# Mamba scan units of one channel chunk by four states, the last image's B products by TensorE and GpSimd, and three quarters of the corner weighting on ScalarE, in a two-layer vision kernel

## The chip, the core and the metric

The kernel runs on one core of a Trainium2 chip. The metric is device time in microseconds of one execution. Engine names as the profile has them: PE is TensorE, PEld its weight loads, DVE is VectorE, ACT is ScalarE, POOL is GpSimd, SP is SyncE (which only issues DMAs here). All arithmetic is float32.

## The reference, cut to what matters

The input is four images of 128 x 128 pixels with 128 channels.

Layer 0, on the group-normalised image: for each of two channel groups, a 3 x 3 convolution gives an offset for each of nine taps; the image is sampled at the nine moved places with bilinear weights (four corners); the 9 x 64 samples go through a depthwise 3 x 3 convolution and a pointwise one to 64 channels. The result is added to the image.

Layer 1, on the group-normalised result: every image row is a sequence of 128 steps for two Mamba layers in a row. One layer, for a sequence, with 256 inner channels d and 16 states n:

```
xz = h @ in_w ; u, res = split(xz)
u = silu(causal_conv4(u) + cb)
dt, B, C = split(u @ xw)
delta = softplus(dt @ dtw + dtb)
h[d,n](t) = exp(delta[d](t) * A[d,n]) * h[d,n](t-1) + delta[d](t) * u[d](t) * B[n](t)
y[d](t) = sum over n of h[d,n](t) * C[n](t) + u[d](t) * D[d]
out = (y * silu(res)) @ ow
```

That result is added too.

## The kernel before, in words

**Order of the work.** `layer0(0)` convolves image 0 alone, and beside it makes the statistics and sampling tables of images 1 to 3 (`todo`). Then the main loop steps two generators: `layer1()`, the Mamba work on image b, and `layer0(b + 1)`, the convolution of the next image. A step of layer 1 is one *unit*; one image has 32 blocks of four rows x 2 layers x 8 units = 512 units. The 288 steps of a layer 0 (32 strips of four rows x nine slot pairs) are spread over all but the last 24 units. Image 3 has Mamba work with no convolution beside it. The program order of this loop goes to a scheduler, which orders each engine's instructions within what the tiles' dependences allow; every engine then works through its own list in order.

**Layer 0, one step** (`gather` and `sample`, lines 347 to 402). Eight indirect DMAs, issued by POOL, fetch for two halves h of two rows each the four corners of 128 pixels for two taps (`gt`, four buffers, two per step). `sample` multiplies each corner by its weight into `gw`: half h = 0 by one DVE tensor_tensor of 128 x 1024 (L387), half h = 1 by 16 ACT activations of 128 x 64 (L382). PE turns and sums the corners into PSUM (`add_transposed`, L128), ACT copies them to one of four `s` buffers (L401), and `add_up` multiplies by the weights on PE (L420). `prep` computes offsets and weights of eight rows (48 times beside layer 1); `table_part` scales the image into the table that is gathered from (`xt`, `xg`; L215, L220).

**Layer 1, the part ahead of a block** (`pre`): projections on PE, `silu` and `softplus` on ACT. At its end four DVE operations of 128 x 1024 (L588 to L591) make delta and du = delta * u. B and C are written to DRAM (`bcd`) so that they can be loaded again, broadcast to all partitions, in `main`.

**Layer 1, one unit, images 0 to 2** (`main`, the `else` branch). A unit is two states (NQ) of both channel chunks (NC), 2,048 elements a partition. SP loads B and C of two states, 128 x 1024 each (`bc`, two buffers each). ACT makes exp(delta * A) with four activations of 128 x 508 (L627) into one of three `da` buffers. DVE makes hs = du * B in two operations of 128 x 1024 (L661), runs the recurrence as one tensor_tensor_scan of 128 x 2048 (L667), and multiplies by C (L670). PE adds the 16 turned pieces into y (L128).

**Layer 1, one unit, image 3** (`in_last`). du is turned by PE (`turn_du`), multiplied by B as a per-partition scalar into `xs`, half by POOL (L646) and half by ACT (L644), turned back by PE into PSUM (`px`, L651), and DVE runs four scans of 128 x 512 that read PSUM (L653) and one multiplication by C (L656).

**End of a block**: DVE multiplies y by silu(res) (L677), PE turns it and projects it, ACT copies.

Of the kernel before, what the change touches and what calls it, by code (L numbers as in the profile page):

```python
# [31 lines left out]
XP = DTR + 1 + 2 * NS  # L32

# [30 lines left out]
def block_kernel(ctx: ExitStack, tc: tile.TileContext, a: dict, out: bass.AP):  # L64
# [26 lines left out]
    pb = ctx.enter_context(tc.tile_pool(name="l0b", bufs=1))  # L91
    ps = ctx.enter_context(tc.tile_pool(name="l0ps", bufs=2, space=PSUM))
    psa = ctx.enter_context(tc.tile_pool(name="l0psa", bufs=2, space=PSUM))
# [3 lines left out]
    psy = ctx.enter_context(tc.tile_pool(name="l1psy", bufs=1, space=PSUM))  # L97

# [6 lines left out]
    offw = loadw("offw", [P, NT, 64])  # L105
# [10 lines left out]
    ones = cw.tile([P, P], F32, name="ones")  # L116
    nc.vector.memset(ones, 1.0)

    wc = cw.tile([P, NT, NT, CG], F32, name="wc")
# [43 lines left out]
    cvw = loadw("cvw", [P, NL, DCONV, NC * P], pool=p2, tag="hs")  # L163
# [7 lines left out]
    xn = cw.tile([P, RB + 2, WP], F32, name="xn")  # L171
    nc.vector.memset(xn, 0.0)

    NSB = 4
    sbuf_s = [cw.tile([P, 4, WP], F32, name=f"s{i}") for i in range(NSB)]
# [5 lines left out]
    def stats_part(b, j):  # L181
        if j == 0:
            stats[b] = small.tile([P, NJ, 6], F32, tag="stats", name=f"stats_{b}")
        xr = pb.tile([P, 4, P], F32, tag="xr", name=f"xr_{b}_{j}", bufs=2)
        nc.sync.dma_start(xr, x[b, 4 * j : 4 * j + 4].rearrange("r w c -> w r c"))
        pt4 = ps.tile([P, 4, P], F32, tag="t", name=f"pt4_{b}_{j}")
        for i in range(4):
            nc.tensor.transpose(pt4[:, i, :], xr[:, i, :], ident)
        nc.vector.bn_stats(stats[b][:, j, :], pt4.rearrange("p r w -> p (r w)"))

    def norm_part(b):
# [3 lines left out]
        for nm, v in (("s", scale), ("b", bias)):  # L195
# [4 lines left out]
            row = small.tile([P, P], F32, tag=f"row_{nm}", name=f"row_{nm}_{b}")  # L200
# [6 lines left out]
    def table_part(b, j):  # L207
# [4 lines left out]
        xt = pb.tile([P, 5, P], F32, tag="xt", name=f"xt_{b}_{j}", bufs=2)  # L212
# [4 lines left out]
        xg = pb.tile([P, G, 5, CG], F32, tag="xg", name=f"xg_{b}_{j}", bufs=1)  # L217
# [150 lines left out]
    def sample(b, j, u, gts):  # L368
# [3 lines left out]
        for h in range(2):  # L372
# [4 lines left out]
            if h:  # L377

                for r in range(2):
                    for s in range(4):  # L380
                        for v in range(2):
                            nc.scalar.activation(  # L382
                                gw[:, r, s, v], gts[h][:, v, r, s * CG : (s + 1) * CG], AF.Copy,
                                scale=wt[:, u, r0 + r, s, v : v + 1],
                            )
            else:
                nc.vector.tensor_tensor(  # L387
                    gw.rearrange("p r s v c -> p (r s) v c"),
                    gts[h].rearrange("p v r (s c) -> p (r s) v c", c=CG),
                    wv.unsqueeze(3).to_broadcast([P, 8, 2, CG]),  # L390
# [75 lines left out]

    NDA = 3
    das = [cw.tile([P, NC, NQ, SR, P], F32, name=f"da{i}") for i in range(NDA)]
    zero = cw.tile([P, NC * NQ * SR], F32, name="zero")
    nc.vector.memset(zero, 0.0)  # L470
    n_da = [0]

# [20 lines left out]
    duts = []  # L493
    n_dut = [0]

    def turn_du(st, nm):

        if not duts:
            duts.append(p2.tile([P, 2, SR, NC * P], F32, tag="hs", name="duts"))
        n_dut[0] += 1  # L500
        dut = duts[0][:, n_dut[0] % 2]
        for k in range(SR // 2):
            pt = ps1.tile([P, 2, NC, P], F32, tag="t", name=f"pdu_{nm}_{k}")
            for i in range(2):
                for c in range(NC):
                    o = (2 * k + i) * P
                    nc.tensor.transpose(pt[:, i, c, :], st["du"][:, c, o : o + P], ident)
            nc.scalar.copy(dut[:, 2 * k : 2 * k + 2], pt.rearrange("p s c d -> p s (c d)"))  # L508
        st["dut"] = dut

    def pre(st, l):

        blk = st["blk"]
        nm = f"{blk}_{l}"
# [45 lines left out]
        if in_last(blk):  # L560

            pbt = ps1.tile([P, SR, XP], F32, tag="t", name=f"pbt_{nm}")
            for i in range(SR):
                nc.tensor.transpose(pbt[:, i, :], dbl[:, i * P : (i + 1) * P], ident[0:XP, 0:XP])
            st["bt"] = p2.tile([P, SR, NS], F32, tag="bt", name=f"bt_{nm}", bufs=2)
            nc.scalar.copy(st["bt"], pbt[:, :, DTR + 1 : DTR + 1 + NS])
# [4 lines left out]
        du = p2.tile([P, NC, TB], F32, tag="du", name=f"du_{nm}", bufs=2)  # L571
# [11 lines left out]
        nc.scalar.activation(du, w1, AF.Ln)  # L583
        nc.scalar.activation(w1, w1, AF.Identity, bias=-1.0)
# [3 lines left out]
        nc.vector.tensor_tensor(e, w1, e, ALU.subtract)  # L588
        nc.vector.tensor_tensor(de, de, e, ALU.subtract)
        nc.vector.tensor_tensor(de, de, du, ALU.add)  # L590
        nc.vector.tensor_tensor(du, de, u, ALU.mult)  # L591
        st.update(u=u, g=g, delta=de, du=du, bcd=bcd)
        st.pop("dut", None)
        if in_last(blk) and duts:
            yield
            turn_du(st, nm)

    def main(st, l):

        blk = st["blk"]  # L600
        nm = f"{blk}_{l}"

        y = psy.tile([P, SR, NC, P], F32, tag="y", name=f"y_{nm}")
# [6 lines left out]
        if in_last(blk) and "dut" not in st:  # L610
            turn_du(st, nm)
        for q in range(NS // NQ):
            bc = []
            for w in range(in_last(blk), 2):
# [208 lines left out]
```

## Time and profile before

| what | us |
|---|---|
| timed runs, median of 3 | 25,891.06 (25,885.81 to 25,894.32) |
| profiled execution, first to last instruction (span) | 24,903.2 |
| difference of the two | 987.9 |
| setup, statistics and table of image 0 | 0 to 273 |
| convolution of image 0 alone | 273 to 3,311 |
| Mamba of images 0 to 2 with convolution of images 1 to 3 | 3,311 to 20,573 |
| Mamba of image 3 | 20,573 to 24,903 |
| busy over the span: PE / DVE / ACT / POOL | 80% / 84% / 65% / 72% |

The timed runs count from start to end of the execution, the span from the first to the last instruction that the profiler recorded; the profiled execution has no timed figure of its own. In the profile a group is all instructions of one line, engine, operation and tiles; it has their number, the busy time, the mean duration in ns, and the time for which the engine stood idle ahead of them, with what ended that idle time. A wait is put down to what came last. POOL's indirect DMAs are counted as busy from issue until their descriptors are out; the data land later.

### The profile page before, as it was taken

How to read it: one execution, taken by the hardware profiler on the slowest of the kernel's cores; microseconds unless marked ns; L12 is line 12 of the kernel's file. 1: busy time of each engine (PE TensorE's matmuls, PEld its weight loads, DVE VectorE, ACT ScalarE, POOL GpSimd, SP SyncE). 2: the span in 40 equal slices, each digit the busy share in tenths (PEclk: the TensorE clock that was granted, in tenths of full speed). 3: DMA queues.
4: the chain of work that ended last, by engine and by line, in shares of the span. 5: the costliest groups of instructions: out<-in, count | busy, mean ns of one | idle time of the engine just before them, and what ended most of it. 6: DMA issues, size and time to landing. Idle time of an engine off the chain costs nothing. (4 is left out here: it accounts for less than half of the span.)

```text
span 24903.2 us, 331178 instructions
## 1 busy us (share of the span) xinstructions
PE 19986.7 (80%) x121156; PEld 13946.7 (56%) x121156; DVE 20935.3 (84%) x13018; ACT 16107.7 (65%) x38037; POOL 17956.4 (72%) x11270
## 2 busy tenths in 40 slices
PE   5788788888888878888888878888888877878877
PEld 3555455555555555555555555555555556666666
DVE  2221269999999999999999999999999998888888
ACT  2444466666666666666666666666666667888887
POOL 4777777887887857788887866787887845555555
PEclk8999989999999888999999888999999889999999
DMA  4554544454444444454544444454454442222221
GB/s 136 157 159 130 151 142 157 156 161 158 158 159 156 158 145 153 157 162 157 159 161 155 159 150 151 153 163 158 159 160 157 157 138 67 69 69 71 70 69 68
DMA packets 1530815, 3471.82 MB, mean 139 GB/s; under 512 B 243283, under 2 KB 717651, under 8 KB 1529052
## 3 DMA queue, kind: packets, MB, share of 16 engines
q1 hardware_dynamic: 1086812, 2242.08, 28.0%
q0 software_dynamic: 442368, 1208.55, 15.4%
q8 instruction: 951, 15.58, 0.3%
q14 instruction: 684, 5.60, 0.1%
HBM read 3299.19 MB, written 150.47 MB: 139 GB/s over the span
## 5 line engine op out<-in xcount | busy, mean ns | idle before, releaser
L359 POOL DMA_INDIRECT gt<-table,idx x9216 | 15606.0, 1693 | 4665.8 <-issue 2582.2
L627 ACT ACTIVATE da<-de,aneg 128x508 f32<-128x508 f32 x8192 | 5455.4, 711 | 2609.2 <-PE y L128 2357.7
L667 DVE TENSOR_TENSOR_SCAN da<-da,hs 128x2048 f32<-128x2048 f32 x1536 | 6792.2, 4422 | 120.2 <-ACT da L627 23.8
L128 PE MATMUL y<-ident,da 128*128 128x128 f32 x32768 | 4753.9, 306 | 2176.1 <-DVE da L670 1901.2
L420 PE MATMUL acc<-s,wc 128*64 128x256 f32 (+3 forms) x38400 | 6060.3, 439 | 276.7 <-ACT s L401 269.1
L128 PEld LDWEIGHTS y<-ident,da 128*128 128x128 f32 x32768 | 4247.0, 159 | 2997.4 <-DVE da L670 2050.8
L382 ACT ACTIVATE gw<-gt,wt 128x64 f32<-128x64 f32 x18432 | 4613.2, 337 | 1024.2 <-DMA gt<-table,idx 592.1
L420 PEld LDWEIGHTS acc<-s,wc 128*64 128x64 f32 x38400 | 3200.8, 140 | 2440.1 <-issue 1287.5
L128 PE MATMUL p<-ident,gw 128*128 128x128 f32 x18432 | 2896.6, 305 | 1471.5 <-DVE gw L387 1215.5
L646 POOL TENSOR_SCALAR xs<-duts,bt 128x256 f32<-128x256 f32 x2048 | 2349.7, 1164 | 2249.2 <-ACT duts L508 1185.7
L661 DVE SCALAR_TENSOR_TENSOR hs<-du,ones,bc 128x1024 f32<-128x1024 f32 x3072 | 3828.0, 1281 | 0.0
L670 DVE SCALAR_TENSOR_TENSOR da<-da,ones,bc 128x2048 f32<-128x2048 f32 x1536 | 3609.6, 2350 | 31.8
L128 PEld LDWEIGHTS p<-ident,gw 128*128 128x128 f32 x18432 | 2363.9, 157 | 2272.0 <-DVE gw L387 1150.1
L387 DVE TENSOR_TENSOR gw<-gt,wt 128x1024 f32<-128x1024 f32 x1152 | 1403.7, 1219 | 2357.9 <-DMA gt<-table,idx 1883.7
L653 DVE TENSOR_TENSOR_SCAN da<-da,px 128x512 f32<-128x512 f32 x2048 | 2350.6, 1202 | 509.2 <-PE px L651 509.2
L401 ACT COPY s<-p 128x512 f32<-128x512 f32 x1152 | 669.7, 581 | 2102.5 <-PE p L128 2100.1
L530 PE MATMUL pu<-hp,inc 128*128 128x512 f32 x4096 | 1830.4, 594 | 1.1 <-ACT ot L700 0.8
L651 PE MATMUL px<-ident,xs 128*128 128x128 f32 x8192 | 1213.5, 287 | 537.8 <-DVE da L653 322.1
L651 PEld LDWEIGHTS px<-ident,xs 128*128 128x128 f32 x8192 | 972.2, 147 | 818.0 <-POOL xs L646 329.3
L530 PEld LDWEIGHTS pu<-hp,inc 128*128 128x128 f32 x4096 | 747.8, 190 | 813.1 <-issue 809.3
L656 DVE TENSOR_TENSOR da<-da,bc 128x2048 f32<-128x2048 f32 x512 | 1172.0, 2289 | 6.6
L644 ACT ACTIVATE xs<-duts,bt 128x256 f32<-128x256 f32 x2048 | 894.3, 499 | 19.3 <-PE px L651 18.8
(133 smaller groups left out, 14768.7 us busy)
## 6 DMA issues: line engine op xcount, KB each, us to landing
bc<-bcd SPq DMA_DIRECT2D x3584, 512.0 KB
gt<-table,idx POOLq DMA_INDIRECT x9216
table<-xg SPq DMA_DIRECT2D x1016, 64.0 KB
xt<-in_x SPq DMA_DIRECT2D x124, 320.0 KB
xr<-in_x SPq DMA_DIRECT2D x128, 256.0 KB
x<-xo SPq DMA_DIRECT2D x128, 256.0 KB
x1t<-x SPq DMA_DIRECT2D x128, 256.0 KB
x1t_o<-x SPq DMA_DIRECT2D x128, 256.0 KB
```

The lines of the kernel that those rows point to most:

```text
L128: nc.tensor.matmul(o, v, ident, is_transpose=True, start=start, stop=stop, skip_group_check=True)
L359: nc.gpsimd.indirect_dma_start(out=gt[:, v, r], out_offset=None, in_=flat, in_offset=bass.IndirectOffsetOnAxis(ap=idx[:, ri, o : o + 1], a ...
L382: nc.scalar.activation(gw[:, r, s, v], gts[h][:, v, r, s * CG : (s + 1) * CG], AF.Copy, scale=wt[:, u, r0 + r, s, v : v + 1],)
L420: nc.tensor.matmul(accs[b, j + i0][CG * g : CG * g + CG, q : q + rb - ra, :], wc[sl, v, e, :], st[p + 4 * g if p < 4 else 8][sl, ra:rb, kx ...
L530: nc.tensor.matmul(px.rearrange("p (s t) -> p s t", s=SR), inc[:, l, j, c * P : (c + 1) * P], h[:, :, j : j + P], start=(j == 0), stop=(j ...
L627: nc.scalar.activation(da[:, c, n, :, 1:], dv[:, :, 1:], AF.Exp, scale=aneg[:, l, c, s : s + 1])
L646: nc.gpsimd.tensor_scalar(xs[:, i], st["dut"][:, i], bv, None, ALU.mult)
L651: nc.tensor.transpose(px[:, i, :], xs[:, i, c * P : (c + 1) * P], ident)
L653: nc.vector.tensor_tensor_scan(dn, dn, px.rearrange("p s t -> p (s t)"), 0.0, ALU.mult, ALU.add)
L661: nc.vector.scalar_tensor_tensor(hs[:, :, n, :], st["du"], ones[:, 0:1], bc[0][:, n].unsqueeze(1).to_broadcast([P, NC, TB]), op0=ALU.mult, ...
L667: nc.vector.tensor_tensor_scan(df, df, hs.rearrange("p c n t -> p (c n t)"), 0.0, ALU.mult, ALU.add)
L670: nc.vector.scalar_tensor_tensor(dc, dc, ones[:, 0:1], cv, op0=ALU.mult, op1=ALU.mult)
```

## The change

**Units of layer 1** are now one chunk by four states (NU) instead of both chunks by two states; there are still eight to a block and layer. hs is one operation of 128 x 2048. B and C are loaded every second unit, 128 x 2048 each, two buffers each. ACT's subtraction of 1 (L584) is folded into the first DVE operation of the preamble, and the product du is made in `make_du`, ahead of the last scan of the block before.

**Corner weighting.** For images 1 to 3 DVE keeps one of the four rows of a step (128 x 512) and ACT takes three (24 activations instead of 16). For image 0 DVE takes all four rows (two operations of 128 x 1024) and ACT none.

**Last image.** du of chunk 0 is reordered into four groups of 32 steps, turned by PE, and 16 matmuls of 32 rows per four states multiply it by a masked B (`make_d` on POOL, `fill` on PE), straight into PSUM; du of chunk 1 is multiplied by the broadcast B on POOL (`times_b`, 128 x 2048). DVE then runs one scan of 128 x 2048 per unit, from PSUM for chunk 0 and from SBUF for chunk 1, and one multiplication by C. The exponentials are made two units ahead in four buffers. B is loaded for this image as well.

**Memory.** The pools of layer 0 lie on the right side and are released ahead of the last image; a pool `first` holds the tables' tiles (`xt` four buffers instead of two, `xg` two instead of one) and is released when layer 1 begins. `s` has three buffers instead of four.

The diff, cut:

```diff
-    NSB = 4
-    sbuf_s = [cw.tile([P, 4, WP], F32, name=f"s{i}") for i in range(NSB)]
+    NSB = 3
+    sbuf_s = [l0w.tile([P, 4, WP], F32, name=f"s{i}") for i in range(NSB)]
...
-        xt = pb.tile([P, 5, P], F32, tag="xt", name=f"xt_{b}_{j}", bufs=2)
+        xt = pp.tile([P, 5, P], F32, tag="xt", name=f"xt_{b}_{j}", bufs=4)
...
-        xg = pb.tile([P, G, 5, CG], F32, tag="xg", name=f"xg_{b}_{j}", bufs=1)
+        xg = pp.tile([P, G, 5, CG], F32, tag="xg", name=f"xg_{b}_{j}", bufs=2)
...
-            if h:
-
-                for r in range(2):
-                    for s in range(4):
-                        for v in range(2):
-                            nc.scalar.activation(
-                                gw[:, r, s, v], gts[h][:, v, r, s * CG : (s + 1) * CG], AF.Copy,
-                                scale=wt[:, u, r0 + r, s, v : v + 1],
-                            )
-            else:
+            alone = 2 if b == 0 else 0 if h else 1
+            for r in range(alone, 2):
+                for s in range(4):
+                    for v in range(2):
+                        nc.scalar.activation(
+                            gw[:, r, s, v], gts[h][:, v, r, s * CG : (s + 1) * CG], AF.Copy,
+                            scale=wt[:, u, r0 + r, s, v : v + 1],
+                        )
+            if alone:
                 nc.vector.tensor_tensor(
...
+                    gw[:, 0:alone].rearrange("p r s v c -> p (r s) v c"),
+                    gts[h][:, :, 0:alone].rearrange("p v r (s c) -> p (r s) v c", c=CG),
+                    wv[:, 0 : 4 * alone].unsqueeze(3).to_broadcast([P, 4 * alone, 2, CG]),
                     ALU.mult,
                 )
...
+    def load_bc(st, u):
+
+        bc = []
+        for w in range(2):
+            t = lm["pool"].tile([P, NU, TB], F32, tag=f"bc{w}", name=f"bc{w}_{st['nm']}_{u}", bufs=2)
+            n0 = w * NS + u * NU
+            nc.sync.dma_start(t, st["bcd"][n0 : n0 + NU, :].partition_broadcast(P))
+            bc.append(t)
+        st["bc", u] = bc
...
-        nc.scalar.activation(du, w1, AF.Ln)
-        nc.scalar.activation(w1, w1, AF.Identity, bias=-1.0)
+        ln = p2.tile([P, NC, TB], F32, tag="yg", name=f"ln_{nm}")
+        nc.scalar.activation(ln, w1, AF.Ln)
...
-        nc.vector.tensor_tensor(e, w1, e, ALU.subtract)
+        nc.vector.scalar_tensor_tensor(e, w1, -1.0, e, op0=ALU.add, op1=ALU.subtract)
         nc.vector.tensor_tensor(de, de, e, ALU.subtract)
-        nc.vector.tensor_tensor(de, de, du, ALU.add)
-        nc.vector.tensor_tensor(du, de, u, ALU.mult)
+        nc.vector.tensor_tensor(de, de, ln, ALU.add)
...
+    def main(st, l, nst, nl):
...
+        for k in range(NC * NS // NU):
+            u, c = divmod(k, NC)
+            if c == 0:
+                load_bc(st, u)
...
+            nc.scalar.copy(da.rearrange("p n s t -> p (n s) t")[:, :, 0], zero)
+            dv = st["delta"][:, c].rearrange("p (s t) -> p s t", s=SR)
+            for i in range(NU):
+                n = u * NU + i
+                nc.scalar.activation(da[:, i, :, 1:], dv[:, :, 1:], AF.Exp, scale=aneg[:, l, c, n : n + 1])
+            hs = lm["pool"].tile([P, NU, TB], F32, tag="hs", name=f"hs_{nm}_{k}")
+            nc.vector.scalar_tensor_tensor(
+                hs, st["du"][:, c].unsqueeze(1).to_broadcast([P, NU, TB]), one, st["bc", u][0],
+                op0=ALU.mult, op1=ALU.mult,
+            )
+            if k == NC * NS // NU - 1 and nst and not in_last(nst["blk"]):
+                make_du(nst)
+            df = da.rearrange("p n s t -> p (n s t)")
+            nc.vector.tensor_tensor_scan(df, df, hs.rearrange("p n t -> p (n t)"), 0.0, ALU.mult, ALU.add)
+            nc.vector.scalar_tensor_tensor(df, df, one, ct, op0=ALU.mult, op1=ALU.mult)
...
+    def make_d(st, u):
+
+        d = le["r"].tile([P, SR, NU, QW], F32, tag="D", name=f"D_{st['nm']}_{u}", bufs=3)
+        nc.gpsimd.tensor_tensor(
+            d, st["bt"][:, :, NU * u : NU * u + NU].unsqueeze(3).to_broadcast([P, SR, NU, QW]),
+            le["mask"].unsqueeze(1).unsqueeze(1).to_broadcast([P, SR, NU, QW]), ALU.mult,
+        )
...
+    def fill(st, u):
+
+        px = le["ps"].tile([P, SR, NU, P], F32, tag="dbu", name=f"px_{st['nm']}_{u}")
+        for q in range(SR):
+            for g in range(SR):
+                o = slice(g * QW, (g + 1) * QW)
+                nc.tensor.matmul(
+                    px[:, g, :, q * QW : (q + 1) * QW],
+                    st["dut"][o, q], st["D", u][o, q],
+                    start=True, stop=True, skip_group_check=True,
+                )
...
+    def times_b(st, u):
+
+        t = le["r"].tile([P, SR, NU, P], F32, tag="dbu", name=f"dbu_{st['nm']}_{u}", bufs=2)
+        nc.gpsimd.tensor_tensor(
+            t, st["du1"].rearrange("p (s t) -> p s t", s=SR).unsqueeze(2).to_broadcast([P, SR, NU, P]),
+            st["bc", u][0].rearrange("p n (s t) -> p s n t", s=SR), ALU.mult,
+        )
...
+    def main_last(st, l, nst, nl):
...
+            hs = le["r"].tile([P, SR, NU, P], F32, tag="he", name=f"he_{nm}_{k}", bufs=3)
+            src = st.pop(("dbu", u)) if c else st["px"]
+            nc.vector.tensor_tensor_scan(
+                hs.rearrange("p s n t -> p (s n t)"),
+                st.pop(("da", k)).rearrange("p s n t -> p (s n t)"),
+                src.rearrange("p s n t -> p (s n t)"), 0.0, ALU.mult, ALU.add,
+            )
+            if c == 0 and nxt[0]:
+                fill(*nxt)
+            nc.vector.tensor_tensor(
+                hs, hs, st["bc", u][1].rearrange("p n (s t) -> p s n t", s=SR), ALU.mult
+            )
...
```

## The prediction

> **What bounds the kernel now.** I read the stages first, then the groups of one stage, then its instructions in order of time. The table by stage (columns: us, then busy time and count of PE, PEld, DVE, ACT, POOL, then clock, DMA share, GB/s) has convolution alone, convolution of images 1 to 3 beside Mamba blocks, and Mamba of the last image:
>
> ```profile
> 273.00:3300.00 3027.00, 2455.94 (x15578) 1546.96 (x15580) 673.52 (x1020) 1345.87 (x5035) 2315.12 (x2314) 0.90 0.50 144
> 3311.00:20573.00 17262.00, 13999.52 (x83687) 9655.16 (x83686) 16357.04 (x8941) 11283.44 (x26768) 13282.61 (x6894) 0.90 0.48 156
> 20573.00:24903.00 4330.00, 3466.47 (x21606) 2703.64 (x21604) 3804.24 (x2876) 3467.19 (x6206) 2349.73 (x2048) 0.93 0.21 69
> ```
>
> The middle stage is 69% of the span and DVE is busy 95% of it. That alone says "shorten DVE". But look at POOL, which issues the gathers. The groups of 500 to 3,100 us, then of 3,800 to 8,600 us (count | busy us, mean ns | idle before):
>
> ```profile
> L359 POOL DMA_INDIRECT gt<-table,idx x1987 | 1990.5, 1002 | 610.9 <-issue 567.6 <-DMA gt<-table,idx 16.5 <-ACT gw L382 14.9
> ...
> L359 POOL DMA_INDIRECT gt<-table,idx x2012 | 3878.8, 1928 | 922.3 <-issue 560.4 <-DVE gw L387 234.2 <-ACT gw L382 82.2
> L667 DVE TENSOR_TENSOR_SCAN da<-da,hs 128x2048 f32<-128x2048 f32 x424 | 1874.9, 4422 | 34.0 <-ACT da L627 7.9 <-DVE hs L661 0.5
> L661 DVE SCALAR_TENSOR_TENSOR hs<-du,ones,bc 128x1024 f32<-128x1024 f32 x847 | 1055.9, 1282 | 0.0
> L670 DVE SCALAR_TENSOR_TENSOR da<-da,ones,bc 128x2048 f32<-128x2048 f32 x423 | 994.1, 2350 | 8.9
> L387 DVE TENSOR_TENSOR gw<-gt,wt 128x1024 f32<-128x1024 f32 x253 | 308.0, 1217 | 199.0 <-DMA gt<-table,idx 186.8 <-PE p L128 12.1
> ```
>
> The same gather instruction takes 1,002 ns beside a quiet DVE and 1,928 ns beside a busy one, and with issue gaps and 316 us of waiting for buffers POOL's 4,800 us are full. The order of time shows why (start us, duration):
>
> ```profile
> 6001.95 2.15 POOL L359 DMA_INDIRECT gt<-table,idx  x1 [0.30 <-issue]
> 6003.19 2.47 DVE L661 SCALAR_TENSOR_TENSOR hs<-du,ones,bc 128x1024 f32<-128x1024 f32 x2
> 6004.40 0.95 POOL L359 DMA_INDIRECT gt<-table,idx  x1 [0.30 <-issue]
> 6005.65 0.95 POOL L359 DMA_INDIRECT gt<-table,idx  x1 [0.31 <-issue]
> 6005.77 4.42 DVE L667 TENSOR_TENSOR_SCAN da<-da,hs 128x2048 f32<-128x2048 f32 x1
> 6006.90 4.04 POOL L359 DMA_INDIRECT gt<-table,idx  x1 [0.30 <-issue]
> 6010.23 2.35 DVE L670 SCALAR_TENSOR_TENSOR da<-da,ones,bc 128x2048 f32<-128x2048 f32 x1
> 6011.25 2.15 POOL L359 DMA_INDIRECT gt<-table,idx  x1 [0.30 <-issue]
> ```
>
> A gather that starts inside a scan ends 0.75 us after the scan (6010.95); one inside L670 ends 0.82 us after it. One that arrives in a seam between two DVE instructions takes 0.95 us. So beside a full DVE **one gather passes per long DVE instruction**, and in DVE idle time one per 0.95 + 0.30 = 1.25 us. Check: those 4,800 us hold 424 + 847 + 423 + 253 such instructions and 53 x 4 of a block's preamble (L588 to L591), 2,159 seams; POOL issued 2,012 and could have issued some 132 more in the 316 us it waited for buffers (2.39 us each), 2,144. DVE instructions with an operand in PSUM do not hold it: xs (L646) took 0.92 us beside the PSUM scans L653 and up to 3.05 us beside L656.
>
> In a sentence apart: the Trainium skill, "SBUF — State Buffer", Who interferes with whom, says a DVE instruction with two SBUF inputs contends with GpSimd's SBUF reads, but also that tensor_tensor was not seen to stall DMA; by the latter the seams would not matter and the sum would be that of rival A; the L387 and L670 rows above decide for the former.
>
> **The change, part by part.**
>
> Middle stage, DVE. hs: two of 1,281 ns become one like L670, 2,350 ns: 212 ns less per unit, 424 x 0.212 = 90 us. gw: 1,024 elements (1,217 ns) become 512; rows of this kind (L220, 320 elements 489 ns; L215, 640 elements 824 ns) give 690 ns, so 253 x 0.53 = 134 us less. The preamble keeps four DVE operations (e as L661's kind, +65 ns x 53 = 3 us). Sum: 4,522 us of DVE work become 4,302.
>
> Middle stage, POOL. For 2,012 gathers the seams are now 424 x 3 + 53 x 4 = 1,484; the 253 gw of 0.69 us end before the next gather is ready (1.25 us after the last seam), so I count them as none. That leaves 528; each needs 1.25 us of DVE idle: 660 us. The bound on the other side counts all 253: 275 x 1.25 = 344 us. The 53 products g (L677, PSUM) pass one each today and later. I take 640 us, near the first end since the row (0.69 against 1.25) is clear. Idle that is not for gathers (278 - 187 = 91 us) stays, of it some hides in the new idle; I keep 91. So 4,302 + 640 + 91 = 5,033 against 4,800, **+233**; bounds -65 (344) and, if POOL's 316 us of buffer waits come on top, +549. The phase has 864 convolution units, 252 in this stretch: x 3.43, so **+800** (-220 to +1,880). After it each image has 24 units without gathers: 72 x 0.21 = -15.
>
> Middle stage, ACT. Eight more pieces per convolution unit; the chain has 16 in 3.93 us, so 8 x 0.246 = 1.97 us x 864, less one 1,044 ns pass (L584) per block: ACT from 65% to about 73%, beside DVE. If that cover is gone, it costs at most 1,700 us. These pieces wait for six of a unit's eight gathers, and queued behind them on ACT are the exponentials that DVE's scans need; three da buffers (some 30 us) cover that.
>
> SP and DMA. B and C come in pairs of 1 MB instead of 0.5 MB, same bytes; a pair's buffer is free two units (20 us) ahead of need, as against one now. Behind a waiting pair on SP stand xw, xs, x1t; PE waits for xs only 2.0 us today. Cost 0; if the 48 image preparations each slipped a unit, 48 x 11 = +530. Three s buffers instead of four: the fourth's reuse already follows add_up in PE's order; 0.
>
> Convolution alone. ACT's 16 pieces become a second gw of 1,226 ns on DVE. ACT's time there hides behind POOL (8 x (1.002 + 0.30) = 10.4 us a unit, 288 units = the 3,027 us), so it returns nothing; the new gw holds gathers. Today 56 ns x 8 = 0.45 us a unit is lost to one gw and the table's operations; I add 0.3 us: **+85** (0 to +300 if each is held 1.05 us). The first table (92 to 272 us) loses 92 us in 30 waits of xg for its stores; SP's 254 issues of 0.43 us (109 us of the 180) bound the relief at 70: **-40**.
>
> Last image. Now 67.7 us per block and layer (4,330/64), 59.4 of it DVE; the rest is mostly L653 waiting for px, hung on POOL's xs. After: 8 x (4.42 + 2.29) + 1.28 + 2.4 + 1.4 + 1.2 = 60.0 us, less 23 overlaps of 0.08 = 58.2. px by PE is 64 matmuls for 128 transposes, so PE (80% now) falls, and so does ACT without xs. What is new is POOL: a product of 2,048 and a mask of 512 elements per four states. The nearest row, xs of 256 elements in 920 ns, bounds 2,048 at 7.4 us if all of it scales; L656 begun 0.2 us after an xs took 2.39 instead of 2.28 us, so xs held DVE only until some 0.47 us after its start, 0.34 us for 256, or 2.7 us for 2,048 and 0.7 for 512. Four pairs: 13.6 us a block if all of it stops DVE (+4.5 us, +290), nothing if it fits beside the PSUM scans of 4.42 us (-9, -580). The product fits by 2.7, the mask hardly: I take 63.8 us, **-250**.
>
> In a sentence apart: the skill's "GPSIMD Engine Reference", Performance versus the Vector engine, gives 4,497 ns for this product, which no row here shows; by it the product just misses the 4.42 us scan and the sum would rise by about 50 us.
>
> Sum: 800 - 15 + 85 - 40 - 250 = **+580 us** on the profiled span of 24,903, so 25,483. The three timed runs (median 25,891.06) are 988 us longer than that span; what lies around it is taken as unchanged: 26,470 us.
>
> **The rivals.**
>
> A, other side, faster: gathers aren't held up. It decides if gathers find as many openings as now (mean of the gather row at most 1.93 us). Then the 220 us per stretch come through: 3.43 x -220 = -755, -15, -250, +45: -975, 24,915 us. For it: DVE's 95%, and only 187 us of waits for gathers now. Against: the seams. 15%.
>
> B, the short gw give seams after all (275 missing): -220 - 15 - 250 + 45 = -440, 25,450. 8%.
>
> C, starved and waiting for buffers too, or ACT late behind gathers: half of 316 us x 3.43 = +540 on the forecast, 27,010; the whole 27,550. For it: gather buffers number only four and 24 of 32 pieces now wait in ACT's queue. 15%.
>
> D, in the last image POOL's products stop DVE in full: +290 instead of -250, 27,010. 7%.
>
> Forecast, 55%, own range 26,100 to 26,900.
>
> **How the numbers follow.** Predicted 26,470. The range 25,400 to 27,450 leaves out A and the far end of C. 0.2% (52 us) is what a measurement can tell from no change. Faster: A, B, 23%, less 1 near zero: 22%; within: 4%; slower: 74%.
>
> **What would show it.** Right: L359's mean rises to about 2.3 us in the middle stage; DVE's busy share there falls to about 85%, with idle before gw or the scans whose releasers are gathers; POOL's waits for buffers shrink. The last stage falls to about 4,080 us, px no longer ends DVE's waits. Wrong: DVE stays at 95% in the middle and L359 at 1.93 (A); or "POOL gt <- ACT gw" grows beyond 316 us a stretch (C); or scans with two SBUF operands last over 5 us in the last image (D).

## The result

The changed kernel took 26,879.89 us (median of 4 runs, 26,855.68 to 26,893.4), beside 25,892.69 us for the kernel before in the same series: ratio 1.0378, 95% interval 1.0364 to 1.0393. It is slower, inside the forecast's range, and by more than the forecast's own step of 580 us.

One thing has to be known to read the numbers below: the kernel before itself took 24,884 us (9 runs) and 24,888 us (15 runs) in two series (runs taken together), and 25,809 to 25,906 us in the others, so totals are compared inside a series, and stages where a series allows it.

The table by stage (us, then busy time and count of PE, PEld, DVE, ACT, POOL, then clock, DMA share, GB/s) of the changed kernel as first profiled, with the same three stages as in the table of the kernel before:

```profile
251.00:4076.00 3825.00, 2622.03 (x15656) 1613.43 (x15657) 1013.19 (x1318) 247.55 (x455) 2424.75 (x2328) 0.81 0.40 115
4076.00:22285.00 18209.00, 14339.81 (x83676) 9689.04 (x83675) 15720.79 (x7408) 12845.43 (x33556) 15251.26 (x6894) 0.88 0.43 148
22285.00:26879.00 4594.00, 3227.97 (x21352) 2463.28 (x21352) 4156.93 (x1404) 2491.52 (x3580) 2127.72 (x507) 0.77 0.33 123
```

All three stages are longer than in the profile of the kernel before (3,027, 17,262, 4,330). That profile goes with the series of some 24,900 us and this one with a higher series: most of the growth of the first stage, and some of the second's, will turn out to be the series. DVE's work in the middle did fall, from 16,357 to 15,721 us, while the stage grew: DVE is busy 86% of it instead of 95%. The groups of 4,600 to 9,400 us, the stretch that answers to 3,800 to 8,600 of the kernel before:

```profile
L365 POOL DMA_INDIRECT gt<-table,idx x1898 | 4143.5, 2183 | 661.3 <-issue 546.2 <-ACT gw L387 87.9 <-ACT da L686 12.2
L695 DVE TENSOR_TENSOR_SCAN da<-da,hs 128x2048 f32<-128x2048 f32 x400 | 1768.8, 4422 | 297.9 <-ACT da L686 163.8 <-issue 101.9 <-ACT gw L387 10.0
L696 DVE SCALAR_TENSOR_TENSOR da<-da,one,bc 128x2048 f32<-128x2048 f32 x399 | 937.6, 2350 | 9.1
L688 DVE SCALAR_TENSOR_TENSOR hs<-du,one,bc 128x2048 f32<-128x2048 f32 x399 | 936.8, 2348 | 0.0
L392 DVE TENSOR_TENSOR gw<-gt,wt 128x512 f32<-128x512 f32 x236 | 160.5, 680 | 289.5 <-DMA gt<-table,idx 173.8 <-remote 79.0 <-PE p L134 18.7
```

The gather's mean rose from 1,928 to 2,183 ns; the scan and the C multiplication kept their durations; POOL's idle time other than issue fell from 362 us (922 - 560) to 115 us (661 - 546). The order of time (start us, duration) shows one unit of three DVE instructions where there were four:

```profile
6015.11 2.34 DVE L696 SCALAR_TENSOR_TENSOR da<-da,one,bc 128x2048 f32<-128x2048 f32 x1
6015.66 2.60 POOL L365 DMA_INDIRECT gt<-table,idx  x1 [0.30 <-issue]
6017.37 2.34 DVE L688 SCALAR_TENSOR_TENSOR hs<-du,one,bc 128x2048 f32<-128x2048 f32 x1
6018.57 1.96 POOL L365 DMA_INDIRECT gt<-table,idx  x1 [0.30 <-issue]
6019.82 4.42 DVE L695 TENSOR_TENSOR_SCAN da<-da,hs 128x2048 f32<-128x2048 f32 x1
6020.84 4.16 POOL L365 DMA_INDIRECT gt<-table,idx  x1 [0.30 <-issue]
```

One gather per DVE instruction, and it ends 0.8 us after the instruction it started beside (6015.66 + 2.60 = 6018.26; L696 ended at 6017.45). The free pair of gathers of 0.95 us that stood between the two hs operations and the scan is gone.

The last image was to fall to about 4,080 us and rose to 4,594. Its DVE groups of 22,285 to 26,879 us:

```profile
L777 DVE TENSOR_TENSOR he<-he,bc 128x2048 f32<-128x2048 f32 x512 | 1564.3, 3074 | 2.2
L770 DVE TENSOR_TENSOR_SCAN he<-dae,dbu 128x2048 f32<-128x2048 f32 x128 | 592.8, 4631 | 0.0
L770 DVE TENSOR_TENSOR_SCAN he<-dae,px 128x2048 f32<-128x2048 f32 x128 | 565.8, 4420 | 423.0 <-PE px L729 399.5 <-ACT da L711 23.5
```

The rows that answer to them in the kernel before, over its last stage:

```profile
L653 DVE TENSOR_TENSOR_SCAN da<-da,px 128x512 f32<-128x512 f32 x2048 | 2350.6, 1202 | 509.2 <-PE px L651 509.2
L656 DVE TENSOR_TENSOR da<-da,bc 128x2048 f32<-128x2048 f32 x512 | 1172.0, 2289 | 6.6
```

The multiplication by C took 3,074 ns instead of 2,289, and px still ends DVE's waits. In the order of time of all engines, both are seen in one place:

```profile
24030.57 8.78 DVE L777 TENSOR_TENSOR he<-he,bc 128x2048 f32<-128x2048 f32 x2
24030.73 6.48 POOL L739 TENSOR_TENSOR dbu<-du,bc 128x2048 f32<-128x2048 f32 x1 [4.36 <-DVE he L770]
24033.45 1.13 PE L578 MATMUL pr<-w_resw,hp 128*128 128x256 f32 x4 [1.48 <-ACT u L573]
24034.51 0.71 PE L729 MATMUL px<-D,dut 32*128 32x128 f32 x12
24037.96 0.69 ACT L573 ACTIVATE u<-pu,w_cvb 128x512 f32<-128x512 f32 x1
24038.70 2.08 PE L578 MATMUL pr<-w_resw,hp 128*128 128x256 f32 x4 [3.47 <-ACT u L573]
24040.71 1.65 PE L729 MATMUL px<-D,dut 32*128 32x128 f32 x20
24042.47 4.42 DVE L770 TENSOR_TENSOR_SCAN he<-dae,px 128x2048 f32<-128x2048 f32 x1 [3.12 <-PE px L729]
```

Two multiplications that take 2.26 us each alone last 8.78 us together beside GpSimd's product. Then the scan waits 3.12 us for a fill whose last 20 matmuls stand on PE behind the next block's residual projection pr (L578), which waits for ACT's u (L573).

### The profile page after: what moved, and what is told of

Same layout as the page of the kernel before. It is cut to its first block, busy times and chain, and to the rows that moved or that the text cites. A ratio compares the mean times of both kernels' runs of the same rounds, so it can differ in the third digit from the quotient of the medians.

```text
span 26879.2 us, 320283 instructions
## 1 busy us (share of the span) xinstructions
PE 20246.2 (75%) x120900; PEld 13801.4 (51%) x120900; DVE 20985.9 (78%) x10302; ACT 15591.2 (58%) x37601; POOL 19804.4 (74%) x9734
## 5 line engine op out<-in xcount | busy, mean ns | idle before, releaser
L365 POOL DMA_INDIRECT gt<-table,idx x9216 | 17650.6, 1915 | 4334.3 <-issue 2644.0
L686 ACT ACTIVATE da<-de,aneg 128x508 f32<-128x508 f32 x6144 | 4048.6, 711 | 545.4 <-PE y L134 509.9
L134 PE MATMUL y<-ident,da 128*128 128x128 f32 x24576 | 3455.2, 297 | 982.5 <-DVE da L696 938.4
L696 DVE SCALAR_TENSOR_TENSOR da<-da,one,bc 128x2048 f32<-128x2048 f32 x1536 | 3613.4, 2352 | 34.9
L688 DVE SCALAR_TENSOR_TENSOR hs<-du,one,bc 128x2048 f32<-128x2048 f32 x1536 | 3611.3, 2351 | 0.0
L392 DVE TENSOR_TENSOR gw<-gt,wt 128x512 f32<-128x512 f32 (+1 forms) x1440 | 1282.3, 897 | 2595.2 <-remote 1386.6
L739 POOL TENSOR_TENSOR dbu<-du,bc 128x2048 f32<-128x2048 f32 x256 | 1420.6, 5561 | 1709.6 <-issue 893.8
L134 PE MATMUL y<-ident,he 128*128 128x128 f32 x8192 | 1365.5, 333 | 799.0 <-DVE he L777 799.0
L134 PEld LDWEIGHTS y<-ident,he 128*128 128x128 f32 x8192 | 1206.3, 175 | 972.5 <-DVE he L777 852.0
L777 DVE TENSOR_TENSOR he<-he,bc 128x2048 f32<-128x2048 f32 x512 | 1564.3, 3074 | 2.2
```

The lines of the kernel that those rows point to most:

```text
L134: nc.tensor.matmul(o, v, ident, is_transpose=True, start=start, stop=stop, skip_group_check=True)
L365: nc.gpsimd.indirect_dma_start(out=gt[:, v, r], out_offset=None, in_=flat, in_offset=bass.IndirectOffsetOnAxis(ap=idx[:, ri, o : o + 1], a ...
L686: nc.scalar.activation(da[:, i, :, 1:], dv[:, :, 1:], AF.Exp, scale=aneg[:, l, c, n : n + 1])
L688: nc.vector.scalar_tensor_tensor(hs, st["du"][:, c].unsqueeze(1).to_broadcast([P, NU, TB]), one, st["bc", u][0], op0=ALU.mult, op1=ALU.mult,)
L696: nc.vector.scalar_tensor_tensor(df, df, one, ct, op0=ALU.mult, op1=ALU.mult)
L739: nc.gpsimd.tensor_tensor(t, st["du1"].rearrange("p (s t) -> p s t", s=SR).unsqueeze(2).to_broadcast([P, SR, NU, P]), st["bc", u][0].rearr ...
```

## The experiments

Theory at the outset: the middle grows because DVE's seams, the openings between its instructions, went missing (so it must shorten again if a seam is put back, even at the price of more DVE work); the last image grows because the product holds DVE, and the fills of px are late because the mask stands behind the product on POOL (so without the product both must go, some 800 us). Rivals: ScalarE's eight more pieces per step make the middle late; PE's fills are late whatever POOL does. Ratios are to the kernel before in the same series, with the 95% interval in brackets.

**The two kernels again**, each in the series of the runs beside it.

> The kernel before, unchanged, for a second profile beside the changed kernel's. Its first profile has a span of 24,903 us, 988 us under its timed runs; the changed kernel's span equals its timed runs. If that first profile was an undisturbed execution of a kind that timed runs are not, this span is near 25,890 us, and a comparison by stage shows where the 988 us sit: all in the stage with convolution alone (then the changed kernel's 3,825 us there, against 3,038, is no effect of the change), or spread over all stages by about 4% (then the middle stage's growth is none either). If the first profile holds, the span is near 24,900 us again and the stages stand as compared.

Measured: 24,903.06 us for the run, span 24,901.3, stages 275, 3,040, 17,269 and 4,317 us: within 13 us of the stages in the prediction. Span and run time agree to 2 us, here and in every other run. So nothing lies "around the span", and the 988 us between the first profile and the first timed runs is a difference between series. Where one stage ends and the next begins is good to some 20 us.

> The changed kernel, unchanged, beside the variants on one chip. The kernel before takes 24,884 us there against 25,892 on the chip of the first result, and in the variants e3 and e4 the stages are 3,043 or 3,130 us (convolution alone), 17,995 (middle), 4,595 (last image). If the chips differ and not the mechanism, this is 25,970 us (250 + 3,126 + 18,000 + 4,595), 4.4% over before, and the 3,825 us of the first changed profile in the convolution alone were the chip's. If that stage is again near 3,800, the second DVE product and the buffers act together, and e3 and e4 each took away one half of the cause.

Measured in another series: 26,842.1 us, ratio 1.0366 (1.0352 to 1.038); stages 249, 3,839, 18,143 and 4,595. The slowdown is the same there. In the series of 24,884 us the changed kernel as a whole was not run; put together from the stages of the runs there that share them (below), it is 249 + 3,130 + 17,998 + 4,595 = 25,972 us, +1,088.

**hs in two.** One more DVE instruction and 212 ns more DVE work per unit:

```diff
-            nc.vector.scalar_tensor_tensor(
-                hs, st["du"][:, c].unsqueeze(1).to_broadcast([P, NU, TB]), one, st["bc", u][0],
-                op0=ALU.mult, op1=ALU.mult,
-            )
+            for i in range(0, NU, 2):
+                nc.vector.scalar_tensor_tensor(
+                    hs[:, i : i + 2], st["du"][:, c].unsqueeze(1).to_broadcast([P, 2, TB]), one,
+                    st["bc", u][0][:, i : i + 2], op0=ALU.mult, op1=ALU.mult,
+                )
```

> The changed kernel with hs made in two operations of two states each, as before, so DVE has 212 ns more work per unit, 325 us in 1,536 units, and one seam more between its instructions. Theory (gathers pass at seams): a unit of the middle stage lacks some 1.2 passes now; one more seam saves 1.25 us of idle time and costs 0.21, so the kernel is 700 to 1,200 us faster, the mean gather in the middle stage falls from 2,183 ns to about 1,930. Rival (ACT's 24 pieces hold back the exponentials, and that bounds the stage): 0 to 325 us slower, gathers as slow as now.

Measured: 24,795.14 us, ratio to before 0.9964 (0.9951 to 0.9976); middle stage 16,805 us against 17,998 in the same series, -1,193; the gather's mean 2,227 to 2,003 ns. Its order of time:

```profile
6002.53 2.15 POOL L365 DMA_INDIRECT gt<-table,idx  x1 [0.30 <-issue]
6003.77 2.48 DVE L689 SCALAR_TENSOR_TENSOR hs<-du,one,bc 128x1024 f32<-128x1024 f32 x2
6004.98 0.94 POOL L365 DMA_INDIRECT gt<-table,idx  x1 [0.30 <-issue]
6006.23 0.95 POOL L365 DMA_INDIRECT gt<-table,idx  x1 [0.30 <-issue]
6006.35 4.42 DVE L696 TENSOR_TENSOR_SCAN da<-da,hs 128x2048 f32<-128x2048 f32 x1
6007.48 4.05 POOL L365 DMA_INDIRECT gt<-table,idx  x1 [0.30 <-issue]
```

The two free gathers are back, and more work on DVE made the stage shorter. ACT's pieces were unchanged, so they alone are not what made it long.

**First image's weighting as before.**

```diff
-            alone = 2 if b == 0 else 0 if h else 1
+            alone = (0 if h else 2) if b == 0 else 0 if h else 1
```

> The changed kernel with image 0's corner weighting as before: one half by DVE, one by 16 ACT pieces; the rest as changed. Theory 1 (the second DVE product of a step, and the table work that queues with it on DVE in order, holds the convolution alone): that stage goes from 3,825 us to about 3,100, the kernel 700 us faster. Theory 2 (the deeper xt and xg buffers let SP issue bursts of loads that delay the gathers' landing): the stage stays near 3,800 us.

Measured: 25,878.64 us, ratio 1.0398 (1.0381 to 1.0415); convolution alone 3,043 us, against 3,126 to 3,130 in the two kernels of that series with two DVE operations there.

**xt and xg as before** (two and one buffers).

> The changed kernel with xt in two buffers and xg in one, as before; the rest as changed. Theory 1 (second DVE product): the stage with convolution alone stays near 3,800 us, or grows as DVE waits longer for xg. Theory 2 (bursts of loads delay the gathers): it falls to about 3,100 us, the kernel 700 us faster.

Measured: 26,001.54 us, ratio 1.0451 (1.0433 to 1.0468); front 275 us as before, where the changed kernel has 246 to 251. The tables of stages in this series confirm the two small terms: the convolution alone costs 83 to 90 us (3,126 to 3,130 against 3,043 in the run above and 3,040 in the kernel before), the first table gains 24 to 29. This run and the one above were to explain the 3,825 us of the first profile; neither theory of theirs holds, since the stage is near 3,100 us here with two DVE operations and in either form of the buffers: most of the excess belongs to the series.

**DVE's part of the weighting as before** (1,024 elements, ACT back to 16 pieces), on the changed kernel.

```diff
-            alone = 2 if b == 0 else 0 if h else 1
+            alone = 2 if b == 0 else 0 if h else 2
```

> The changed kernel with the corner weighting beside Mamba as before, DVE 128x1024 for one half and 16 ACT pieces for the other; the merged hs stays. Theory (seams): 0.53 us more DVE work per convolution unit, but a gw of 1.22 us is long enough to give a pass where one of 0.69 us gives none: 0.59 passes per Mamba unit, worth 0.74 us against 0.31, so the middle stage is about 630 us shorter (400 to 800), still some 100 us longer than before's 17,269. Rival 1 (ACT's pieces hold back the exponentials): the whole excess of 730 us and the saving on hs come back, 1,000 us shorter. Rival 2 (DVE's work alone counts): 460 us longer.

Measured: 26,655.59 us, ratio 1.0293 (1.0277 to 1.0308); middle 17,972 against 18,143 in its series, -171. The direction is right and the size is a miss. Its groups of 4,600 to 9,400 us:

```profile
L695 DVE TENSOR_TENSOR_SCAN da<-da,hs 128x2048 f32<-128x2048 f32 x407 | 1799.5, 4421 | 74.6 <-ACT da L686 42.4 <-PE y L134 4.3 <-issue 2.9
L392 DVE TENSOR_TENSOR gw<-gt,wt 128x1024 f32<-128x1024 f32 x241 | 293.1, 1216 | 371.7 <-DMA gt<-table,idx 325.4 <-PE p L134 20.1 <-PE pdt L616 13.3
```

The scans' wait for ACT's da fell from 163.8 to 42.4 us a stretch, and the gw's wait grew from 289.5 to 371.7: with ScalarE relieved, the wait for the gathers only changed its place. DVE's idle time fell from 704 to 509 us, by 195 where 241 x 1.25 = 301 would go with the theory: at 1.25 us each, 156 of 241 longer gw let a gather pass. Those that start out of an idle wait for their own gather add no opening; that this is why the rest failed is argued, not shown.

**GpSimd's product of the last image left out** (chunk 1 then scans a constant).

```diff
-        t = le["r"].tile([P, SR, NU, P], F32, tag="dbu", name=f"dbu_{st['nm']}_{u}", bufs=2)
-        nc.gpsimd.tensor_tensor(
-            t, st["du1"]...
-        )
+        if "keep" not in le:
+            le["keep"] = le["r"].tile([P, SR, NU, P], F32, name="keep")
+            nc.gpsimd.memset(le["keep"], 0.5)
+        t = le["keep"]
```

> The changed kernel without POOL's product of B and du for chunk 1 in the last image (a constant tile stands in its place, so that half of that image's states is left out). Theory (the product holds DVE's second operand port): the multiplications by C fall from 3,087 to about 2,290 ns (6.4 us a block), and the mask, no longer queued behind the product, lets PE fill px in time (6.3 us a block of waits): 12.7 x 64, 800 us less, last stage near 3,800 us. Rival (PE's fill itself is late): only the 410 us of the multiplications come back, the waits for px stay.

Measured: 26,805.43 us, ratio 1.0348 (1.0332 to 1.0364); last image 4,547 us against 4,595, only -48. The wait (DVE's waits in the last stage):

```profile
DVE he L769 <- PE px L729: 677.3, 118, 7.4
```

It was 399.5 us with the product. DVE's busy time fell by 333 us (4,157 to 3,824), and the longer wait took most of it back: the product was not the last obstacle, and the theory's 800 us did not come. What is left of the hold (multiplications of 2,482 ns on the mean, 2,289 in the kernel before) goes with POOL's mask, which this run keeps.

**All fills by PE**, in two halves of 128 x 1024, no product on GpSimd (with hs in two and the first image's weighting as before).

> A version meant to beat both: hs in two operations; image 0's weighting as before; in the last image both chunks' B products by PE from the same mask, in two px tiles of two sequences each, the scan in two halves, and POOL making only the mask. Theory: convolution alone 3,043, middle 16,800 as in e2, last image 59 us of DVE a block plus 8 x 0.2 for the split scan and 1 to 2 us of waits, 62 us, 3,970: 24,060 us in all where before takes 24,884, a ratio of 0.967. Rival (the fills of the split scan are late, 1.5 us a unit): last image 4,700, 24,800 us, no gain.

Measured: 26,075.23 us, ratio 1.0064 (1.005 to 1.0078); middle 16,900, last image 4,913 us with 1,063.9 us of waits for px. Twice the fills on PE doubled and more the waits for them, and the stage is longer than the rival's 4,700 us. Both runs pointed at PE's order, so a theory took shape: the fills are late because of what stands ahead of them in PE's queue, pr behind ACT's u above all.

**The residual projection later.** Only in the last image, pr and its Silu are traced behind the softplus:

```diff
+        def gate():
+
-        for i in range(SR // 2):
+            for i in range(SR // 2):
...
+        if not in_last(blk):
+            gate()
         yield
...
         nc.scalar.activation(ln, w1, AF.Ln)
+        if in_last(blk):
+            gate()
         yield
```

> The changed kernel, in the last image's blocks with the residual projection pr and its Silu g of the next block traced behind the softplus's Ln instead of right behind u, so that no projection that waits for ScalarE's u stands ahead of the fills of px in TensorE's queue. Everything else as in the changed kernel; the middle and the convolution alone should not move. In the changed kernel's last stage (4,595 us, 64 blocks, 71.8 us each) VectorE waits for px at the fifth scan of a block (3.1 us per block) and at the first scan of the next (3.6 us per block). Theory 'queue': the wait at the fifth scan is the fill standing behind pr, so it goes (64 x 3.1 = 200 us), and the one at the block's seam shrinks if the next block's fill comes earlier too (up to 64 x 3.6 = 230 us more): last stage 4,170 to 4,420 us, the kernel 175 to 425 us shorter than the changed one. Rival 'port': VectorE and the fills are late because GpSimd's products hold VectorE, and a wait that goes at one place comes back at another, as when the product was left out: last stage 4,550 us or more.

Measured: 26,541.1 us, ratio 1.0282 (1.0265 to 1.0299); last image 4,358 us, -237; middle 18,150. DVE's waits in the last stage:

```profile
DVE he L778 <- PE px L737: 79.7, 62, 1.4
```

399.5 became 79.7 us, with no wait over 1.4 us, and PE's idle time ahead of pr, waiting for u, fell from 332 to 4 us. As expected, 'queue'. Not all of the 320 us was gained: DVE's busy time in the stage grew from 4,157 to 4,257 us, since DVE and POOL's work now meet more often (among them a scan of dbu that lasted 5.26 us instead of 4.41 beside the mask).

**Both: the residual projection later and no product.**

> As the kernel with the late residual projection, and GpSimd's product of du and B for chunk 1 in the last image left out (a constant tile stands in its place, so that chunk's scans run on wrong numbers). Without the late projection, leaving the product out gained only 48 us, because the wait for px took its place. Theory 'queue': with the fills no longer late, the product's hold on VectorE shows in full: the C multiplication at 3,086 ns instead of 2,289 ns is 8 x 0.8 = 6.4 us per block, 64 x 6.4 = 410 us at most; expected 250 to 410 us below the kernel with the late projection, last stage 3,830 to 4,050 us (VectorE's own instructions alone are 59.7 us per block, 3,820 us). Rival: something other than pr keeps the fills late (the chain of du, its transposition and the copy), and the stage gains less than 120 us by it again.

Measured: 26,179.97 us, ratio 1.0147 (1.013 to 1.0164); last image 3,997 us, -361 against the run above. The same edit that had gained 48 us gains 361 once the wait behind it is gone. Hold and wait are two causes, and each hid the other.

**The edits together**: hs in two, first image's weighting as before, pr late.

> The changed kernel with the three edits that the runs so far point to: the middle's product in two instructions of two states each (one more seam per unit for the gathers), the first image's weighting as in the kernel before, and the last image's residual projection behind the softplus. Stages measured one by one: front 246 to 250 us, convolution alone as before, middle 16,805 to 16,900 us (17,270 before), last stage 4,360 us (4,317 before): sum 24,900 - 27 - 465 (or 370) + 43, so 370 to 450 us under the kernel before, ratio 0.982 to 0.987. Theory 'stages add': the ratio is in that range. Rival: the last stage's late projection or the first image's weighting collides with the longer gather chain, and the ratio is 0.990 or more.

Measured: 24,460.74 us (5 runs), 24,887.96 before (15 runs), ratio 0.9828 (0.9815 to 0.9841). By stage:

```profile
248.00:3281.00 3033.00, 2457.66 (x15658) 1550.59 (x15658) 675.15 (x1030) 1356.21 (x5062) 2325.62 (x2323) 0.90 0.50 145
3281.00:20107.00 16826.00, 13861.17 (x83673) 9479.86 (x83671) 15904.75 (x8942) 12755.78 (x33534) 13809.56 (x6900) 0.92 0.46 160
20107.00:24465.00 4358.00, 3116.14 (x21352) 2344.78 (x21352) 4256.12 (x1406) 2582.12 (x3643) 2021.78 (x506) 0.80 0.34 129
```

The stages add, and this kernel is 1.7% faster than the kernel before: the middle gains 443 us on it (17,269), the front 27, and the last image still loses 41 (4,317).

**All fills by PE, with pr late.**

> As the kernel with units in two, first image's weighting as before and the late residual projection, but in the last image both chunks' products of du and B are made by TensorE's fills (in halves), and GpSimd makes none. Without the late projection this form took 4,913 us in the last stage, with 884 us of waits for px in 4,000. Theory 'queue': about half of those waits were fills behind pr and behind the pieces that wait for u; GpSimd no longer holds VectorE (361 us with the late projection); TensorE is then the bound, busy 60 us per block (3,340 us in 4,000 over 55.7 blocks) of 64: last stage 4,050 to 4,350 us, at or below the kernel with the products (4,358 us). Rival 'TensorE's order': the fills stand behind the transposed additions and the input projection whatever pr does, and the last stage is 4,500 us or more.

Measured: 24,841.47 us, ratio 0.998 (0.9971 to 0.9989); last image 4,749 us. The rival 'TensorE's order' holds here. DVE's waits in the last stage and the stage itself:

```profile
DVE he L774 <- PE px L742: 772.6, 299, 7.5
```

```profile
20088.00:24837.00 4749.00, 3911.39 (x29796) 3070.80 (x29796) 3807.18 (x1918) 2609.28 (x3706) 317.92 (x253) 0.82 0.17 63
```

DVE's busy time is as low as in the kernel before (3,807 us; 3,804 there) and PE's is high (3,911 us; only the first run with all fills by PE has more, 4,092). While DVE waited for px, PE was at work: some 330 us on the fills themselves, 255 on the output projection, 150 on the transposed additions, 90 on pr. Moving pr took 291 us of waits (1,063.9 to 772.6), not half, and DVE waited 138 us for ACT's w, where it had not waited before.

## Why the prediction was right or wrong

**The rule of the seams: right.** With one gather per DVE instruction (the 128 x 512 gw counted as none) and 1.25 us of idle DVE for each that finds no opening, a stretch of the changed kernel has 400 + 399 + 399 + 4 x 50 = 1,398 openings for 1,898 gathers, so 500 x 1.25 = 625 us; DVE was idle 4,800 - 4,096 = 704. In the run with hs in two, 440 + 878 + 439 + 4 x 55 = 1,977 openings stand for 1,961 gathers, none is missing, and DVE was idle 256 us. That the short gw gives no opening is seen in the changed kernel's order of time: the gather begun at 6010.27 lasts 5.10 us, over a scan (to 6014.61) and the gw behind it (6014.52 to 6015.19). With a gw of 1.22 us the rule promises too much: in that run 156 of 241 let a gather pass.

**Middle stage, +800 less 15: right.** 17,998 against 17,269 in one series: +729 (+747 from the first scan of this stage to the first of the last image). DVE's busy share (86%, 85% forecast) and the gather's mean (2.18 to 2.23 us, 2.3 forecast) moved as stated. Rival A needed the mean to stay at 1.93, and B a stage 220 us shorter. Of rival C, ACT's da did end 164 us of waits a stretch, but taking eight pieces off ACT only moved the wait to the gathers.

**Convolution alone, +85, and the first table, -40:** measured +83 to +90 (in the series of 24,884 us) and -24 to -29: right.

**Last image, -250: wrong; it measured +275 to +278** (+259 to +263 from its first scan on). Per block and layer the account is 4,594 / 64 = 71.8 us where I had 63.8. DVE's own work: 58.3 us (58.2 forecast). The hold: (3,074 - 2,289) x 512 + (4,631 - 4,416) x 128 = 429 us, 6.7 a block (5.6 forecast, because of an estimate of 2.7 us for a product that takes 4.51 us at least). The wait for px and da: 423 us, 6.6 a block; forecast nothing. So the hold was mis-sized by 1.1 us, and the step that failed is the sentence that the rest of the old 67.7 us is DVE "waiting for px, hung on POOL's xs", and goes with xs. The kernel before shows what ended that wait, in its order of time:

```profile
23093.24 3.60 PE L530 MATMUL pu<-hp,inc 128*128 128x512 f32 x8
23096.67 1.91 PE L128 MATMUL y<-ident,da 128*128 128x128 f32 x16
23098.42 3.60 PE L530 MATMUL pu<-hp,inc 128*128 128x512 f32 x8
23101.86 1.47 PE L651 MATMUL px<-ident,xs 128*128 128x128 f32 x12
23102.56 2.33 DVE L653 TENSOR_TENSOR_SCAN da<-da,px 128x512 f32<-128x512 f32 x2 [6.67 <-PE px L651]
```

In the block shown 6.67 us, of 8.0 on the mean (509.2 / 64), stand behind PE's input projection pu, not behind xs. The whole stage says the same: in the 509 us PE was on pu for some 340, and stood idle for xs for less than 3. The wait belonged to the order of PE's queue, and in the changed kernel the fills again stood behind other work there: in the 399.5 us of its waits PE was on the fills themselves for some 215, on y for 100, on pr for 95 and on the turning of du for 35. I read the releaser's name and PE's falling load, and not the queue in front of it. The run with pr late shows that the order decided (waits 399.5 to 79.7 us); that the old wait would have gone the same way was not tried. A slower PE is not seen in it: the granted clock of the stage is 0.77, beside 0.93 in the kernel before, but eight matmuls of pu take 3.60 us in both.

**Rival D, +290 here, came near by its number, and by luck.** It had the products stop DVE for 13.6 us a block, which makes 58.2 + 13.6 = 71.8, the time measured. But the hold was half of that, and the wait for px, which D did not have, the other half. (The prediction's bounds of +290 and -580 do not quite follow from its own 58.2: they would be +260 and -610.)

In a sentence apart: the Trainium skill's figure in "GPSIMD Engine Reference", Performance versus the Vector engine, 4,497 ns for an addition of this size, agrees with the 4,511 ns of the shortest product here, and would have been the better entry for the hold.

**The 988 us "around the span": wrong as a cause.** Every run has a span within 2 us of its own time. It was the distance of two series. That the forecast's total came near (26,470 for 26,880) rests on adding it to a span of one series to compare with runs of another, which is the right sum for a wrong reason: luck. In the higher series the changed kernel's convolution alone takes 640 to 720 us more (3,763 to 3,847 against 3,126 to 3,130), the middle some 140 to 210 us more, the last image the same. With the first image's weighting as before, the convolution alone took 4,024 us in a higher series (the run with all fills by PE) against 3,029 to 3,043: some 990 us, about the whole difference of the kernel before. So the edit that costs 83 to 90 us in one kind of series saved some 200 in the other. In the convolution alone of the changed kernel the DMA engines moved 115 GB/s in the higher series; in the other:

```profile
275.00:3405.00 3130.00, 2485.64 (x15658) 1545.08 (x15658) 1023.37 (x1318) 245.59 (x455) 2422.18 (x2323) 0.88 0.48 140
```

Here the work is that of the changed kernel's first stage (x1318 on DVE, x455 on ACT). What makes a series high stays open: one chip by its number had both kinds, and no profile of the kernel before was taken in a high one.

Summed by stages in one series, against its profile of the kernel before: 729 + 90 - 26 + 278 = +1,071 us against +580 forecast, 491 missed. The last image alone missed by 528; the other terms gave 37 back.

## What to carry to other kernels

Where GpSimd issues indirect DMAs beside a busy VectorE, count VectorE's instructions, not only their time: merging two operations saved 212 ns a unit and cost the gathers an opening, and splitting them again took 1,193 us off the stage. When a wait is to go, look at what stands ahead of its releaser in that engine's own queue; the name of the releaser tells who was last, not why. And when leaving out a suspected cost gains little, look for the wait that took its place before you acquit it: the same edit was worth 48 us and then 361.

## What the runs showed of the hardware that was not expected

- GpSimd's tensor_tensor and VectorE's stop each other over long stretches: a multiplication of 2.26 us lasted up to 6.62 us, the product of 4.51 us up to 6.65, and scans with both operands in SBUF up to 5.27 instead of 4.41, while scans that read PSUM kept 4.41 to 4.42 us beside it.
- A tensor_tensor holds a gather as the scan does: in the kernel before, a gather begun 0.06 us after a tensor_tensor of 1.21 us (L588, at 6016.14) lasted 1.96 us, to 0.81 us after that instruction's end, where the free ones took 0.95.
- The same kernel before took 24,884 us in one series and 25,906 in another with nothing changed. In the changed kernel 640 to 720 us of such a difference are in the stage that waits for gathers with little else to do.
